# Layer 0 of a two-layer kernel from unit 48 on: engine queues in the source's order, and short consumer steps dealt out over units

## The chip, the cores and the metric

The kernel runs on one core of a Trainium2 chip. The metric is device time in microseconds (us) of one execution, from start to end of the program, as the median of several runs. A profiled execution has a span of its own (first to last recorded instruction), which is used where the working goes into the trace.

## The reference

Two layers act on an input x of 4 batches of 512 tokens with 512 features, held in 16 bits. Each layer normalises x, computes an attention-like branch s and a gate branch g from the normalised input, and adds s * silu(g) to x:

```python
xn = _layernorm(x)
s = _L0_attn_ref(xn, Wq, Wk, Wv, Wo)
g = _silu(_L0_ffn_ref(xn, SU_ug, SU_dp, Wscale_ug, Wscale_dp, W_up, W_gate, W_down))
x = x + s * g
xn = _layernorm(x)
s = _L1_attn_ref(xn, ...)
g = _silu(_L1_ffn_ref(xn, ...))
x = x + s * g
```

Only the first layer is touched by the change. Its two branches are:

```python
# attention: 32 heads of 16 features, 8 key/value heads (4 query heads share one)
attn = jnp.einsum('bhqd,bhkd->bhqk', q, k) * scale
attn = jax.nn.softmax(attn, axis=-1).astype(jnp.float16)
out = jnp.einsum('bhqk,bhkd->bhqd', attn, v)
return out.transpose(0, 2, 1, 3).reshape(b, s, 512) @ Wo
...
# feed-forward: 512 -> 2048 -> 512, with Walsh-Hadamard transforms before both products
x = fwht(x * SU_ug) / SCALE
x_up = x @ W_up.T * (Wscale_ug[:INTER] * SCALE)
x_gate = x @ W_gate.T * (Wscale_ug[INTER:] * SCALE)
x = jax.nn.silu(x_gate) * x_up
x = fwht(x * SU_dp) / SCALE
return x @ W_down.T * (Wscale_dp * SCALE)
```

The second layer is a gated delta-rule recurrence over the tokens with a feed-forward of sign weights.

## The kernel before

**Units.** Layer 0 is dealt out in 256 units (NU, L379): 4 batches x 8 sets x 8 units; a set is the four query heads that share one key/value head, so a batch takes 64 units, and "unit 27 of a batch" means u % 64 = 27. The loop at L544 runs over units and issues for each of them, in this order, what is due:

- *values* (L454), once in eight units: the weighted sum of the values of a whole set, in 16 matmuls from the exponentials into one PSUM bank, a ScalarE copy `os`, and then the chain of *attention sums*: the row sums go out to memory and come back as 128 rows (`rc`), are inverted on VectorE, go out (`rec_d`) and come back spread over all rows (`sm`, four DMAs); GpSimd multiplies `os` by `sm` into `oT`, and four DMAs sort its rows into `oTc`, from which the output product reads. Transfers here are issued by SyncE.
- *maxima* (L422): two matmuls (L429) give scores in `sc`, and VectorE takes the negated row maxima `nmx` (L430).
- *exps* of the unit 11 earlier (LAG): two matmuls with the keys on the rows (L450) into `st`, and ScalarE's exponential `pe` (L452).
- two *halves* of the feed-forward, which trails by 16 units (LATE): 32 units (16 to 47 of the attention's count) compute gate and up products (`gate_up`, L323: "gate units", eight L333 matmuls each; the weights `wc`, four buffers, are loaded by SyncE), the next 32 compute the output product (`down`, L346: "down units", two L351 matmuls each). After a gate product ScalarE takes its tanh `th` and VectorE forms (th + 1) * gate (L340); after an up product ScalarE copies it to `hT` (L343) and GpSimd multiplies the two (L344).
- `max_rows` at the end of a set (L432): VectorE splits the maxima in a 16-bit value and its remainder (`nm`), TensorE transposes them (L439), and VectorE adds them to the queries as two more rows (`qm`, L441), so that the second score product has the maximum already subtracted.
- steps that come once or twice a batch: `queries` (L387), `set_queries` (L412), `layer_sum` of the batch before (L488, four: output product, gate `sg`, sum `x1`), `norm1` (L499, four: statistics of x1 with the first, then normalise, transpose, store), the load and statistics of the next batch's x (`load_x`, `stats0`), its `norm0` (L144, four: normalise, transpose on TensorE, two ScalarE copies `xnT` and `xr`), `keys` (L289) and `values_of` (L303, four). In `norm0` and `norm1` the first of the four also takes the inverse standard deviations: add on VectorE, square root on ScalarE (L68), reciprocal on VectorE.

**PSUM.** `sc` and `st` are one buffer each (two banks), `mm` has three banks and holds the feed-forward's sums; `y` is a single bank, shared by everything else. In a gate unit `keys`, values and `values_of` may take an `mm` bank (`either`, L368) where the feed-forward piece is below 32 of its batch; otherwise they too take `y`.

**Order.** Each engine executes its own queue in order. The order inside a queue is not that of the source: a scheduler in the tile framework places the instructions, by its own estimates of when operands and buffers are ready, unless an instruction is pinned by `keep_in_program_order`, which is used here only for the start (`inorder`, L131) and in layer 1. DMAs are issued from the queue of the engine on which they are called, mostly SyncE (SP).

**Into layer 1.** The feed-forward of the last batch is not done when the units end. What is left of it, and the last batch's `layer_sum` and `norm1`, form the list `rest` (L585), of which entries are dealt out between the steps of layer 1's first batch in proportion to the work done (L876). After them layer 1's own constants are set up; among them `osc` and `drow` come by DMAs from ScalarE's queue (L889 to L895) and are used on VectorE (L902).

Of the kernel before, what the change touches and what calls it, by code (L numbers as in the profile page):

```python
# [18 lines left out]
P = 128  # L19
# [12 lines left out]

@with_exitstack
def kernel(ctx: ExitStack, tc: tile.TileContext, i: dict, out: bass.AP):
    nc = tc.nc
# [18 lines left out]

    def ln_params(pool, rows, tag):

        n = len(rows)
        mv = new(pool, [P, n, 2], F32, tag + "mv")
        for k, r in enumerate(rows):
            st = new(pool, [P, 6], F32, tag + "st")  # L60
            nc.vector.bn_stats(st, r)
            nc.vector.bn_aggr(mv[:, k, :], st)
        return mv, inv_std(pool, mv, n, tag)

    def inv_std(pool, mv, n, tag, pin=lambda ins: ins):
        rstd = new(pool, [P, n], F32, tag + "rs")
        pin(nc.vector.tensor_scalar(rstd, mv[:, :, 1], EPS, None, ALU.add))
        pin(nc.scalar.activation(rstd, rstd, AF.Sqrt))  # L68
        pin(nc.vector.reciprocal(rstd, rstd))
        return rstd  # L70
# [21 lines left out]
    make_identity(nc, identf)  # L92
    ident16 = new(cst, [P, P], F16, "ident16")
    make_identity(nc, ident16)
# [6 lines left out]
    if True:  # L101
# [40 lines left out]
        rstds = {}  # L142

        def norm0(b, pin=lambda ins: ins, then=lambda: None, tiles=range(TB)):  # L144
            xin, mv = xins[b], lnp[b]
            if 0 in tiles:
                xnTs[b] = new(b0, [P, KC, SEQ], F16, "xnT")
                xrs[b] = new(hp, [P, KC, SEQ], F32R, "xr", bufs=1)
                rstds[b] = inv_std(b0, mv, TB, "ln", pin)
            xnT, rstd = xnTs[b], rstds[b]  # L150
            then()
            for t in tiles:
                xn = new(b0, [P, DM], F16, "xn")
                pin(normalize(xn, xin[:, t, :], mv, rstd, t))
                pt = new(bmm, [P, KC, P], F16, "mm") if b == 0 else new(bpy, [P, KC, P], F16, "y")
                for k in range(KC):
                    nc.tensor.transpose(pt[:, k, :], xn[:, ts(k, P)], ident16)
                pin(nc.scalar.copy(xnT[:, :, ts(t, P)], pt))
                if b > 0:
                    nc.scalar.copy(xrs[b][:, :, ts(t, P)], pt)  # L160
            if b == 0:
                for t in range(TB):
                    pin(nc.scalar.copy(xrs[b][:, :, ts(t, P)], xnT[:, :, ts(t, P)]))
# [1312 lines left out]
```

## Time and profile before

| | |
|---|---|
| Median of three runs (1486.90, 1487.87, 1488.85) | 1487.87 us |
| Profiled execution: its time / its span | 1496.22 / 1494.5 us |
| Mean granted TensorE clock of it | 0.985 |
| TensorE busy (matmuls) | 1429.8 us, 96% |
| VectorE busy | 1033.9 us, 69% |
| ScalarE busy | 710.6 us, 48% |
| GpSimd busy | 314.5 us, 21% |
| Memory traffic, mean over the span | 129 GB/s |

The page's groups of instructions list the costliest lines with busy time, mean duration of one, and the idle time of the engine just before them with what ended it. For layer 0 the largest are:

```profile
L430 DVE TENSOR_REDUCE nmx<-sc 128x2 f32<-128x1024 f32 x256 | 312.2, 1220 | 141.3 <-PE st L450 136.2
L452 ACT ACTIVATE pe<-st 128x1024 f16<-128x1024 f32 x256 | 262.6, 1026 | 134.2 <-PE st L450 132.2
L351 PE MATMUL mm<-wdn,hT 128*128 128x512 f32 x512 | 254.4, 618 | 0.0
L333 PE MATMUL mm<-xr,wc 128*128 128x512 f32 x768 | 208.4, 413 | 0.5 <-DMA wc<-wS 0.5
```

A line such as the first reads: line 430, VectorE, a reduction from `sc` to `nmx`, 256 of them, 312.2 us together and 1220 ns each; VectorE had been idle for 141.3 us before them, mostly until a matmul at L450 ended. Idle time of an engine that does not set the pace costs nothing. In the views by time, `PE`, `PEld`, `DVE`, `ACT`, `POOL` and `SP` are TensorE's matmuls, its weight loads, VectorE, ScalarE, GpSimd and SyncE; "[0.47 <-ACT pe]" at the end of a line means that the engine had waited 0.47 us for an ACT instruction on the tile `pe`; in a list of waits stand total, count and the longest. Layer 0 takes the span up to about 830 us; unit 48 starts at about 185 us.

### The profile page before, as it was taken

To read this page: it belongs to the slowest core of one execution; us is meant where nothing else is said; L and a number is where in the kernel's file an instruction comes from. 1 tells how busy PE (TensorE), PEld (TensorE's weight loads), DVE (VectorE), ACT (ScalarE), POOL (GpSimd) and SP (SyncE) were. 2 spreads that over 40 slices of the span, in tenths; PEclk is the share of its full clock that TensorE was granted. 3 is DMA by queue.
4 is the path that set the end of the run, shared out by engine and by line. 5 is a ranking of instruction groups with operands and counts; after the bars stand their busy time and mean duration, and the time that the engine had idled before them with its cause. 6 is when DMAs were issued, how large, how long until landed. Compare 5 with 4: busy or idle time off the path is not lost. (4 is left out here: it accounts for less than half of the span.)

```text
span 1494.5 us, 22672 instructions
## 1 busy us (share of the span) xinstructions
PE 1429.8 (96%) x8144; PEld 859.7 (58%) x8144; DVE 1033.9 (69%) x1863; ACT 710.6 (48%) x1046; POOL 314.5 (21%) x304
## 2 busy tenths in 40 slices
PE   7999999999999999999999699999999999999998
PEld 3456543465335653366335476787568765776675
DVE  7799855756557655676516769668975799477746
ACT  4555554566446664466443434434353344323433
POOL 1022200322003210133110230045112531052001
PEclk9899999999999999999999899999999999999989
DMA  8856310465105640166012543434453354425532
GB/s 294 319 198 227 115 58 23 147 238 191 27 24 201 224 143 27 59 227 222 20 51 80 155 138 106 120 88 137 140 153 105 91 161 135 125 71 148 165 83 96
DMA packets 201793, 199.11 MB, mean 133 GB/s; under 512 B 65520, under 2 KB 153040, under 8 KB 200784
## 3 DMA queue, kind: packets, MB, share of 16 engines
q1 hardware_dynamic: 198624, 196.29, 41.5%
q10 hardware_dynamic: 3056, 1.37, 0.4%
q8 instruction: 64, 1.05, 0.3%
q14 instruction: 49, 0.40, 0.1%
HBM read 146.80 MB, written 46.19 MB: 129 GB/s over the span
## 5 line engine op out<-in xcount | busy, mean ns | idle before, releaser
L430 DVE TENSOR_REDUCE nmx<-sc 128x2 f32<-128x1024 f32 x256 | 312.2, 1220 | 141.3 <-PE st L450 136.2
L452 ACT ACTIVATE pe<-st 128x1024 f16<-128x1024 f32 x256 | 262.6, 1026 | 134.2 <-PE st L450 132.2
L351 PE MATMUL mm<-wdn,hT 128*128 128x512 f32 x512 | 254.4, 618 | 0.0
L333 PE MATMUL mm<-xr,wc 128*128 128x512 f32 x768 | 208.4, 413 | 0.5 <-DMA wc<-wS 0.5
L333 PEld LDWEIGHTS mm<-xr,wc 128*128 128x128 f32 x768 | 138.4, 190 | 49.7 <-issue 22.0
L344 POOL TENSOR_TENSOR hT<-hT,th 128x512 f32<-128x512 f32 x64 | 85.3, 1333 | 317.1 <-ACT hT L343 285.8
L351 PEld LDWEIGHTS mm<-wdn,hT 128*128 128x128 f32 x512 | 86.7, 189 | 90.8 <-issue 90.1
L729 PE MATMUL pu<-xn1T,wp 128*128 128x512 f32 x288 | 131.0, 598 | 0.0
L959 PE MATMUL ph<-xsh,sg 128*128 128x512 f32 x256 | 112.8, 441 | 5.6 <-ACT sg L944 5.3
L429 PE MATMUL sc<-kT,qT 32*128 32x512 f16 x512 | 104.4, 388 | 4.8 <-DVE nmx L430 4.5
L944 ACT ACTIVATE sg<-sw 128x512 fp32r<-128x512 f32 x128 | 79.5, 625 | 56.7 <-PE y L990 29.1
L959 PE MATMUL ph<-xsl,sg 128*128 128x512 f32 x256 | 104.1, 407 | 0.7 <-DVE xsl L919 0.7
L450 PE MATMUL st<-qm,kT 32*128 32x512 f16 x512 | 102.8, 388 | 1.6 <-ACT pe L452 1.6
L476 POOL TENSOR_TENSOR oT<-os,sm 128x512 f16<-128x512 f32 x32 | 41.5, 1297 | 284.7 <-DMA sm<-rec_d 253.1
L429 PEld LDWEIGHTS <-qT 32*128 32x128 f16 x512 | 26.5, 91 | 119.4 <-issue 112.4
L964 ACT ACTIVATE hT<-ph,upsc 128x512 f32<-128x512 f32 x64 | 43.9, 686 | 95.6 <-PE ph L959 95.4
L729 PEld LDWEIGHTS pu<-xn1T,wp 128*128 128x128 f32 x288 | 54.2, 192 | 57.3 <-issue 55.6
L990 PE MATMUL y<-sg,hsh 128*128 128x512 f32 x256 | 82.9, 432 | 0.9 <-ACT sg L944 0.9
L333 PE MATMUL mm<-xr,fo 128*128 128x512 f32 x256 | 75.9, 431 | 0.6 <-DVE fo L260 0.5
L1037 POOL TENSOR_TENSOR gm<-g,le 128x384 fp32r<-128x384 f32 x64 | 57.2, 911 | 89.2 <-PE pu L1038 58.8
L990 PE MATMUL y<-sg,hsl 128*128 128x512 f32 x256 | 73.5, 400 | 0.0
L339 ACT ACTIVATE th<-mm,hwg 128x512 f32<-128x512 f32 x64 | 44.1, 689 | 52.3 <-PE mm L333 49.0
(307 smaller groups left out, 2368.8 us busy)
## 6 DMA issues: line engine op xcount, KB each, us to landing
wc<-wS SPq DMA_DIRECT2D x96, 512.0 KB
wS<-fo SPq DMA_DIRECT2D x16, 1024.0 KB
sw<-in_upT SPq DMA_DIRECT2D x64, 256.0 KB
sw<-in_downT SPq DMA_DIRECT2D x64, 256.0 KB
sm<-rec_d SPq DMA_DIRECT2D x128, 64.0 KB
raw<-in_w_gateT SPq DMA_DIRECT2D x8, 512.0 KB
hT<-in_w_downT SPq DMA_DIRECT2D x16, 256.0 KB
raw<-in_w_upT SPq DMA_DIRECT2D x8, 512.0 KB
```

The source lines that it names most:

```text
L333: nc.tensor.matmul(pgs[m], wcs[b, c, m][:, h, k, :], xrs[b][:, k, :], start=(k + h == 0), stop=(k == KC - 1 and h == 1))
L344: nc.gpsimd.tensor_tensor(hT, hT, ths[b, c], ALU.mult)
L351: nc.tensor.matmul(ys[t], hTs[b, c][:, ts(t, P)], wdn[:, c, :], start=(c == 0), stop=(c == NI - 1))
L429: nc.tensor.matmul(sc[:, j, :], qTs[n][rows, ts(t, P)], kTs[b, g // 4][rows, :], start=True, stop=True)
L430: nc.vector.tensor_reduce(nmxs[n][:, t, 2 * pr : 2 * pr + 2], sc, AX.X, ALU.max, negate=True)
L450: nc.tensor.matmul(st[:, j, :], kTs[b, g // 4][rows, ts(k, P)], qms[n][rows, :], start=True, stop=True)
L452: nc.scalar.activation(pes[u], st, AF.Exp)
L729: nc.tensor.matmul(pp, wps[b, n][:, k, 0:P], xn1Ts[b][:, k, :], start=(k == 0), stop=(k == KC - 1))
L944: tc.keep_in_program_order(nc.scalar.activation(sgs[b, c, m], raws[b, c, m], AF.Sign))
L959: ins = nc.tensor.matmul(ph, sgs[b, c, 0][:, ts(k, P)], xss[b][n][:, k, :], start=(k + n == 0), stop=(k == KC - 1 and n == 1))
L990: ins = nc.tensor.matmul(yss[b][t], hss[b, c][n][:, ts(t, P)], sgs[b, c, 1], start=(c + n == 0), stop=(c == NI - 1 and n == 1))
L1037: nc.gpsimd.tensor_tensor(gm, bc_in(s["g2"][:, t, u, x], P), bc_mid(le, 3), ALU.mult)
```

## The change

From unit 48 on (`FIRST`), every instruction that the unit loop calls on TensorE, VectorE, ScalarE and GpSimd is pinned to the source's order, by a wrapper around the engines (`InOrder`, on while `ordered[0]`); SyncE's DMA issues stay free, and the pinning ends with the loop. The steps of the loop are cut smaller, and what consumes a TensorE or DMA result is deferred by `later(n, f)`, which runs f in the unit n later, after that unit's exps and before its values and feed-forward:

- by one unit: the gate product (th + 1) * gate, the final gate product of `down`, the copies `kd` (with its DMAs), `vp` and `xr`, the addition `qm`, and of `layer_sum` everything after the matmuls (not for the last batch);
- the attention sums in three parts: `os`, its DMA out and `rc` in at once, the reciprocal with `rec_d` and `sm` three units later, the product `oT` with its DMAs five units later;
- `max_rows` is split: the maxima in 16 bits and remainder stay at the end of the set, the transposes (`query_rows`) go to the end of the next unit, `qm` to the one after;
- `norm0` is split in a root (unit 47 of a batch), scale steps (48 to 51) and turns (49 to 52), one a unit; `norm1` in statistics (21 to 24), root (25), scale steps (26 to 29) and turns (27 to 30);
- `queries` moves by one unit (22, 23 of 32), `layer_sum` from 17-20 to 18-21, `keys` from 52 to 53, `values_of` from 56-59 to 57-60; values stands behind exps instead of ahead of maxima.

The list `rest` has the same work in 38 entries instead of 29. No arithmetic is added or left out. The core of the diff:

```diff
+class InOrder:
+    def __init__(self, tc, engine, on):
+        self.tc, self.engine, self.on = tc, engine, on
+    def __getattr__(self, name):
+        f = getattr(self.engine, name)
+        if not self.on[0]:
+            return f
+        return lambda *args, **kw: self.tc.keep_in_program_order(f(*args, **kw))
+class Engines:
+    def __init__(self, tc, on):
+        nc = tc.nc
+        self.tensor, self.vector, self.scalar, self.gpsimd = (
+            InOrder(tc, e, on) for e in (nc.tensor, nc.vector, nc.scalar, nc.gpsimd)
+        )
+        self.sync = nc.sync
 @with_exitstack
 def tile_two_layers_kernel(ctx: ExitStack, tc: tile.TileContext, i: dict, out: bass.AP):
-    nc = tc.nc
+    ordered = [False]
+    nc = Engines(tc, ordered)
...
+        def root(pool, mv, n, tag, pin=lambda ins: ins):
+            rstd = new(pool, [P, n], F32, tag + "rs")
+            pin(nc.vector.tensor_scalar(rstd, mv[:, :, 1], EPS, None, ALU.add))
+            pin(nc.scalar.activation(rstd, rstd, AF.Sqrt))
+            return rstd
+        def norm0_root(b, pin=lambda ins: ins):
+            rstds[b] = root(b0, lnp[b], TB, "ln", pin)
+        def norm0_scale(b, t, pin=lambda ins: ins):
+            if t == 0:
+                pin(nc.vector.reciprocal(rstds[b], rstds[b]))
                 xnTs[b] = new(b0, [P, KC, SEQ], F16, "xnT")
                 xrs[b] = new(hp, [P, KC, SEQ], F32R, "xr", bufs=1)
-                rstds[b] = inv_std(b0, mv, TB, "ln", pin)
-            xnT, rstd = xnTs[b], rstds[b]
-            then()
-            for t in tiles:
-                xn = new(b0, [P, DM], F16, "xn")
-                pin(normalize(xn, xin[:, t, :], mv, rstd, t))
-                pt = new(bmm, [P, KC, P], F16, "mm") if b == 0 else new(bpy, [P, KC, P], F16, "y")
-                for k in range(KC):
-                    nc.tensor.transpose(pt[:, k, :], xn[:, ts(k, P)], ident16)
-                pin(nc.scalar.copy(xnT[:, :, ts(t, P)], pt))
-                if b > 0:
-                    nc.scalar.copy(xrs[b][:, :, ts(t, P)], pt)
-            if b == 0:
-                for t in range(TB):
-                    pin(nc.scalar.copy(xrs[b][:, :, ts(t, P)], xnT[:, :, ts(t, P)]))
+            xns[b, t] = new(b0, [P, DM], F16, "xn")
+            pin(normalize(xns[b, t], xins[b][:, t, :], lnp[b], rstds[b], t))
+        def norm0_turn(b, t, pin=lambda ins: ins):
+            pt = new(bmm, [P, KC, P], F16, "mm") if b == 0 else new(bpy, [P, KC, P], F16, "y")
+            for k in range(KC):
+                nc.tensor.transpose(pt[:, k, :], xns[b, t][:, ts(k, P)], ident16)
+            pin(nc.scalar.copy(xnTs[b][:, :, ts(t, P)], pt))
+            if b > 0:
+                later(1, lambda: nc.scalar.copy(xrs[b][:, :, ts(t, P)], pt))
...
+        waiting, unit = {}, [0]
+        def later(n, f):
+            waiting.setdefault(unit[0] + n, []).append(f)
...
+            def place():
+                kd = new(b0, [P, SEQ], F16, "kd", bufs=1)
+                nc.vector.tensor_copy(kd, pk)
+                for v in range(2):
+                    kT = kTs[b, v] = kTz[2 * (b % 2) + v]
+                    if b + v == 0:
+                        continue
+                    for j in range(4):
+                        nc.sync.dma_start(kT[32 * j + 2 : 32 * j + 2 + HD0, :], kd[ds(64 * v + HD0 * j, HD0), :])
+            later(1, place) if b else place()
...
+                def place(t=t, pv=pv):
+                    nc.vector.tensor_copy(
+                        vp[:, t, :, 0:HD0], pv[:, : NKV * HD0].rearrange("p (h d) -> p h d", d=HD0)
+                    )
+                later(1, place) if b else place()
...
-                nc.scalar.activation(th, pgs[0], AF.Tanh, scale=hwg[:, c : c + 1])
-                nc.vector.scalar_tensor_tensor(th, th, 1.0, pgs[0], ALU.add, ALU.mult)
+                pg = pgs[0]
+                nc.scalar.activation(th, pg, AF.Tanh, scale=hwg[:, c : c + 1])
+                later(1, lambda: nc.vector.scalar_tensor_tensor(th, th, 1.0, pg, ALU.add, ALU.mult))
...
-                nc.scalar.activation(th, ys[t], AF.Tanh, scale=0.5)
-                nc.vector.scalar_tensor_tensor(g0s[b][:, t, :], th, 1.0, ys[t], ALU.add, ALU.mult)
+                y, g = ys[t], g0s[b][:, t, :]
+                nc.scalar.activation(th, y, AF.Tanh, scale=0.5)
+                later(1, lambda: nc.vector.scalar_tensor_tensor(g, th, 1.0, y, ALU.add, ALU.mult))
...
-        NU, LAG, LATE = 8 * len(sets), 11, 16
+        NU, LAG, LATE, FIRST = 8 * len(sets), 11, 16, 48
...
+        def query_rows(n):
+            nmg = nms[n % 2]
             pm = misc(F16)
             for t in range(TB):
                 nc.tensor.transpose(pm[:, ts(t, P)], nmg[:, t].rearrange("p j d -> p (j d)"), ident16)
             qms[n] = new(b0, [P, SEQ], F16, "qm")
-            nc.vector.tensor_tensor(qms[n], pm, qTs[n], ALU.add)
+            later(1, lambda: nc.vector.tensor_tensor(qms[n], pm, qTs[n], ALU.add))
...
+            def invert():
+                nc.vector.reciprocal(rc, rc)
+                nc.sync.dma_start(rec_d[b, g].rearrange("j (p x) -> (j p) x", p=32), rc)
+                for j in range(4):
+                    nc.sync.dma_start(sm[32 * j : 32 * j + 32, :], rec_d[b, g, j : j + 1, :].to_broadcast([32, SEQ]))
+            def place():
+                oT = new(hp, [P, SEQ], F16, "oT")
+                nc.gpsimd.tensor_tensor(oT, os_, sm, ALU.mult)
+                v, r = g // 4, g % 4
+                for j in range(4):
+                    if r == 0 and j % 2 == 0:
+                        oTs[b, 2 * v + j // 2] = new(hp, [P, SEQ], F16, "oTc", bufs=6)
+                    nc.sync.dma_start(
+                        oTs[b, 2 * v + j // 2][ds(64 * (j % 2) + HD0 * r, HD0), :], oT[32 * j : 32 * j + HD0, :]
+                    )
+            later(3, invert)
+            later(5, place)
...
+            def place():
+                sg = new(zp[0], [P, DM], F32, "sg")
+                nc.vector.scalar_tensor_tensor(sg, ps, 0.5, g0s[b][:, t, :], ALU.mult, ALU.mult)
+                x1 = x1s[t] = new(zp[0], [P, DM], F32, "x1", bufs=4)
+                nc.gpsimd.tensor_tensor(x1, sg, xins[b][:, t, :], ALU.add)
+                nc.sync.dma_start(x1_d[tok, :], x1)
+            later(1, place) if b < NB - 1 else place()
...
+        def stats1(b, t):
             if t == 0:
-                mvs[b] = ln_params(zp[0], [x1s[n] for n in range(TB)], "ln")
-            xn1 = new(zp[0], [P, DM], F32, "xn1")
-            normalize(xn1, x1s[t], *mvs[b], t)
+                mvs[b] = new(zp[0], [P, TB, 2], F32, "lnmv")
+            s6 = new(zp[0], [P, 6], F32, "lnst")
+            nc.vector.bn_stats(s6, x1s[t])
+            nc.vector.bn_aggr(mvs[b][:, t, :], s6)
+        def norm1_root(b):
+            rstds[b, 1] = root(zp[0], mvs[b], TB, "ln")
+        def norm1_scale(b, t):
+            if t == 0:
+                nc.vector.reciprocal(rstds[b, 1], rstds[b, 1])
+            xn1s[t] = new(zp[0], [P, DM], F32, "xn1")
+            normalize(xn1s[t], x1s[t], mvs[b], rstds[b, 1], t)
+        def norm1_turn(b, t):
             pt = misc()
             for k in range(KC):
-                nc.tensor.transpose(pt[:, ts(k, P)], xn1[:, ts(k, P)], identf)
+                nc.tensor.transpose(pt[:, ts(k, P)], xn1s[t][:, ts(k, P)], identf)
...
+            if h >= halves(NU + LAG + 1):
+                settle()
+        def settle():
+            for n in sorted(waiting):
+                for f in waiting.pop(n):
+                    f()
...
+            unit[0] = u
+            ordered[0] = u >= FIRST
             if v == 32:
...
-            if 0 < u - LAG <= NU and (u - LAG) % 8 == 0:
-                values((u - LAG) // 8 - 1)
             if u < NU:
                 maxima(u)
             if 0 <= u - LAG < NU:
                 exps(u - LAG)
+            for f in waiting.pop(u, ()):
+                f()
+            if 0 < u - LAG <= NU and (u - LAG) % 8 == 0:
+                values((u - LAG) // 8 - 1)
             for f in early.get(u, ()):
                 f()
             for h in range(halves(u), halves(u + 1)):
                 half(h)
             if u % 8 == 7 and u < NU:
                 max_rows(u // 8)
-            if u % 32 in (21, 22) and u + 11 < NU:
-                queries((u + 11) // 64, (u + 11) % 64 // 32, u % 32 - 21)
+            if u % 8 == 0 and 0 < u <= NU:
+                query_rows(u // 8 - 1)
+            if u % 32 in (22, 23) and u + 10 < NU:
+                queries((u + 10) // 64, (u + 10) % 64 // 32, u % 32 - 22)
             if u % 8 == 0 and u + 8 < NU:
                 set_queries(u // 8 + 1)
             if 16 <= v < 16 + NI:
                 fold_down(v - 16)
-            if 0 < b < NB and r in (17, 18, 19, 20):
-                layer_sum(b - 1, r - 17)
-            if 0 < b < NB and r in (25, 26, 28, 29):
-                norm1(b - 1, (25, 26, 28, 29).index(r))
+            if 0 < b < NB and r in (18, 19, 20, 21):
+                layer_sum(b - 1, r - 18)
+            if 0 < b < NB:
+                if 21 <= r < 25:
+                    stats1(b - 1, r - 21)
+                if r == 25:
+                    norm1_root(b - 1)
+                if 27 <= r < 31:
+                    norm1_turn(b - 1, r - 27)
+                if 26 <= r < 30:
+                    norm1_scale(b - 1, r - 26)
             if b + 1 < NB:
                 if r == 34:
                     load_x(b + 1)
                 if r in (43, 44, 45, 46):
                     stats0(b + 1, r - 43)
+                if r == 47:
+                    norm0_root(b + 1)
+                if 49 <= r < 53:
+                    norm0_turn(b + 1, r - 49)
                 if 48 <= r < 52:
-                    norm0(b + 1, tiles=(r - 48,))
-                if r == 52:
+                    norm0_scale(b + 1, r - 48)
+                if r == 53:
                     keys(b + 1)
-                if 56 <= r < 60:
-                    values_of(b + 1, (r - 56,))
+                if 57 <= r < 61:
+                    values_of(b + 1, (r - 57,))
+        ordered[0] = False
+        settle()
         rest = [(half, h) for h in range(halves(NU + LAG + 1), 2 * NU)]
...
-        rest += [(f, NB - 1, t) for f in (layer_sum, norm1) for t in range(TB)]
+        rest += [(layer_sum, NB - 1, t) for t in range(TB)]
+        rest += [(stats1, NB - 1, t) for t in range(TB)]
+        rest.append((norm1_root, NB - 1))
+        for t in range(TB):
+            rest += [(norm1_scale, NB - 1, t), (norm1_turn, NB - 1, t)]
```

## The prediction

> **What bounds the kernel now.** I read the page first (PE is busy 96% of the span), then the busy time of each engine in stretches cut at every sixteenth row maximum (L430), which makes stretches of 16 units. Of those lines four are enough; after the length of the stretch stand PE, PEld, DVE, ACT and POOL busy, the granted clock, and the DMA share with GB/s.
>
> ```profile
> 363.70:407.80 44.10, 44.04 (x214) 17.69 (x215) 25.01 (x34) 24.01 (x31) 4.64 (x4) 1.00 0.14 43
> 407.80:446.40 38.60, 38.59 (x170) 13.87 (x170) 22.84 (x27) 18.60 (x21) 3.60 (x4) 1.00 0.08 23
> 446.40:500.30 53.90, 50.66 (x272) 30.31 (x271) 38.29 (x64) 34.67 (x46) 15.14 (x13) 0.97 0.59 195
> 675.00:716.40 41.40, 41.40 (x233) 25.69 (x233) 26.06 (x33) 26.31 (x34) 12.84 (x11) 1.00 0.56 189
> ```
>
> Units 112-127 (first line; they hold all of norm0, keys and values_of), 128-143 and 224-239 leave TensorE idle for 0.06 us at most: no order of the queues can shorten them. Only units such as 144-159 (third line; layer_sum and norm1) lose time, and there the clock is also below 1. What can be won is what TensorE waits for from unit 48 on; the whole list of its waits from 185 to 752 us:
>
> ```profile
> PE y L439 <- DVE nm L436: 4.9, 4, 1.8
> PE st L450 <- ACT pe L452: 1.4, 3, 0.6
> PE sc L429 <- DVE nmx L430: 1.0, 1, 1.0
> PE mm L333 <- DMA wc<-wS: 0.5, 2, 0.3
> PE y L284 <- DVE qm L441: 0.2, 1, 0.2
> ```
>
> That is 8.0 us. To it comes the clock; in two stretches of the same view it is half:
>
> ```profile
> 295.06:298.47 3.41, 1.69 (x10) 1.19 (x11) 3.41 (x5) 1.18 (x2) 1.26 (x1) 1.00 0.10 24
> 298.48:301.89 3.41, 3.41 (x12) 1.94 (x11) 1.58 (x5) 3.02 (x5) 0.00 (x0) 0.50 0.73 279
> 475.97:479.38 3.41, 3.41 (x12) 2.12 (x11) 1.40 (x4) 2.38 (x4) 0.00 (x0) 0.50 0.59 201
> 783.12:786.53 3.41, 1.89 (x7) 0.84 (x6) 0.17 (x1) 0.21 (x1) 0.23 (x1) 1.00 0.72 203
> ```
>
> A stretch of 3.41 us with 1.72 us idle (first line) is followed by one at clock 0.50; one with 1.52 us idle (last line; the clock stays 1) is not. Eight L333 matmuls took from 475.70 to 479.20 us at half clock and from 479.59 to 481.57 at full: 3.5 against 2.0, so a half-clock stretch costs 1.5 us. **The most that layer 0 can give back is 8.0 + 2 x 1.5 = 11 us.**
>
> **The change, part by part.** The built program confirms that from unit 48 on each of the four engines follows the source: TensorE runs maxima(u), exps(u-11), values where due, the unit's feed-forward, then the rest; ScalarE exp, due copies, then the copies of this unit's results. SyncE stays free. No work is added except two more table loads in layer 1 (31 instead of 29). So I looked where a first-in-first-out queue now waits.
>
> Unit lengths: two values and two query_rows cost 2 x (0.98 + 0.33) = 2.6 us per 16 units (timeline: values 413.57 to 414.55, transposes L439 to the next matmul 0.33). A down unit is (38.60 - 2.6)/16 = 2.25 us, a gate unit (41.40 - 2.6)/16 = 2.42 us; the four attention matmuls at its head take 0.32 of it. About 0.1 us passes between a producer's last matmul and its reader.
>
> (a) *Sqrt in a pinned ScalarE queue.* Before, the scheduler moved TensorE work into the hole:
>
> ```profile
> 464.87 1.28 ACT L68 ACT_TABLE_LOAD   x1
> 467.41 1.28 ACT L452 ACT_TABLE_LOAD   x1
> 468.49 0.39 PE L429 MATMUL sc<-kT,qT 32*128 32x512 f16 x2
> 468.81 0.50 PE L333 MATMUL mm<-xr,wc 128*128 128x512 f32 x1
> 469.78 0.39 PE L450 MATMUL st<-qm,kT 32*128 32x512 f16 x2 [0.47 <-ACT pe L452]
> ```
>
> Gate work (L333) stands between maxima (L429) and exps (L450), and TensorE lost 0.47 us. Pinned, norm1_root stands at unit 25 of a batch behind the copy hT: 0.1 + 0.59 (L343) + 1.28 + 0.21 (L68) + 1.28 + 1.03 (L452) = 4.49 us after that unit's matmuls `st` is free again. TensorE asks for it in exps of unit 27, one gate unit (2.42) later, and waits 2.1 us with all feed-forward work behind it; three batches: 6.3. norm0_root at unit 47: 4.49 - (2.25 + 0.33) = 1.9 us in unit 49; two batches (the first root, in unit 47, is not pinned): 3.8. The DVE sums feeding Sqrt end earlier (row maximum 1.22, then at most 1.4 more). Sum 10.1 us.
>
> [...]
>
> (b) *One `y` bank, unit 51.* Before:
>
> ```profile
> 370.79 0.59 ACT L158 COPY xnT<-y 128x512 f16<-128x512 f16 x1 [0.46 <-PE y L157]
> 371.00 1.13 PE L351 MATMUL mm<-wdn,hT 128*128 128x512 f32 x2
> 371.27 0.59 ACT L160 CAST xr<-y 128x512 fp32r<-128x512 f16 x1
> 371.75 1.04 ACT L452 ACTIVATE pe<-st 128x1024 f16<-128x1024 f32 x1
> 372.06 1.05 PE L460 MATMUL y<-pe,vp 128*32 128x512 f16 x16
> ```
>
> xr follows xnT at once, and values comes after one of the unit's two down matmuls, so nothing waits. After, xr is due one unit later and behind exp, and values stands ahead of the down matmuls. From the unit's start: 0.1 + 0.59 + 1.03 + 0.59 = 2.3 us until `y` is free, TensorE is there at 0.32: it waits 2.0 us, three batches: 6.0.
>
> (c) *The same bank, unit 59.* The copy vp of the previous unit's values_of is due after this unit's row maximum: 0.45 + 1.22 + 0.29 (L315) = 1.96, less 0.32: 1.65 us, three times: 5.0.
>
> (d) *layer_sum in unit 21.* The bank is freed by sg (L494, 0.69) behind the row maximum and the gate product th (0.67): 0.45 + 1.22 + 0.67 + 0.69 = 3.03, TensorE is there at 2.42: 0.6 x 3. Unit 22's queries wait 0.2 x 2. In units 19 and 20 the longer PE work or the missing th hides it. Sum 2.2.
>
> (e) *Small.* Turns in units 50 and 52 and keys in 53 find `y` free at 2.35 instead of 2.25 (0.1 each); queries in 54 wait for kd behind the reciprocal: 0.45 + 1.22 + 0.24 + 0.69 = 2.6, 0.35. Three batches: 2.0.
>
> (f) *Half clock.* The waits of (a) and (b), eight in all, are 1.9 to 2.1 us long, more than the 1.72 that halved the clock, but must lie almost within one stretch of 3.41 us. I take three, 4.5 us; bounds 0 and 8 x 1.5 = 12.
>
> [...] The row at 295.06 says that 1.7 us is enough.
>
> (g) *Split maxima.* The transposes L439 come one unit after nm, so the 4.9 us go; stats0 no longer runs into norm1, and gate work no longer splits maxima from exps. I credit the full 11 us.
>
> (h) *Attention sums.* They stretch from 12.2 us (os copy to last oTc issue, quiet units) to the fixed five units. For a batch's last set invert is in unit 14, the product in 16; layer_sum reads it at the end of 18. After the reciprocal: rec_d 0.3, landing 1.4, four sm issues 1.75, landing 1.8, product 1.27, four oTc issues 2.4, landing 1.7: 10.6 us. From reciprocal (unit 14, 1.9 us) to the last layer_sum matmul there are 12: covered by 1 us; uncovered it costs its lateness, up to 1.5 us, three times. On SyncE, wc loads for units 27 to 30 stand behind these oTc in unit 25: issued some 2.6 us into it, needed 6.1 us into it, plus the 2.1 us of (a). Taken as 0, bounds 0 and 6.
>
> (i) *Start of layer 1.* The final halves, layer_sum and norm1 are dealt out over 38 entries instead of 29, so they come sooner.
>
> ```profile
> 836.80 1.12 PE L506 MATMUL mm<-identf,xn 128*128 128x128 f32 x8 [4.40 <-DVE xn L73]
> 856.20 1.12 PE L753 MATMUL pu<-identf,yv 128*128 128x128 f32 x4 [5.64 <-DVE yv L742]
> ```
>
> The first wait is DVE's (16.65 of 17 us busy from 825 to 842); its work is only reordered. The second holds 3.19 us in which DVE waited at L902 for osc, whose DMA ScalarE now issues one projection earlier. Gain 3; bounds: 10 lost waits (gain 10), and two more loads of 1.28 with the order against us (loss 4). The rest of layer 1 keeps its order.
>
> Sum: 10.1 + 6.0 + 5.0 + 2.2 + 2.0 + 4.5 - 11 - 3 = **+15.8 us**. It is made against the profiled execution (span 1494.5, its time 1496.2), which ran 8.3 us over the median 1487.9; I carry the difference over: **1503.7 us**.
>
> **Rivals.** *Layer 1 pays for it (faster).* Speaks for it: the two waits above with their 0.72 and the half-clock stretches behind them (5.24 against 3.60 us for eight L729) are worth 4.4 + 0.7 + 5.6 + 2 x 3.4 = 17.5 us, and the halves come sooner. Against: DVE is full there. If all of it went and no clock halved in layer 0: 25.3 - 11 - 17.5 = -3 us, 1485. It decides from a gain of 14 there on. Chance 0.08.
> *The waits overlap (no change).* If half of (a) to (e) hid behind work that I put on the path, 12.6 + 1.5 - 14 = 0, 1488. Against: each wait heads a queue with everything behind it. Chance 0.06. It is also the time if the pinning moved nothing.
> *Half clock everywhere, SyncE late.* (f) at 12 and (h) at 3: +26, 1514. For: the waits exceed 1.72. Against: stretches and waits must line up. Chance 0.16.
> My forecast: 0.70, with its own range 1497 to 1511.
>
> **The numbers.** Within 0.2% (3 us) a measurement of this kernel cannot tell from no change. Slower 0.70 + 0.16 = 0.86, same 0.06, faster 0.08. The range 1494 to 1514 leaves out about 2 in 10.
>
> **What would show it.** After: waits of PE for pe of about 2 us, eleven a run in units 27, 49 (pe), 51 (xr) and 59 (vp), and nm gone from the list; stretches of 16 units near 44 + 6.5 where norm0 stands and unchanged 38.6 and 41.4 elsewhere; clock 0.5 after some of the waits; osc no longer before 856. I am wrong if units 49, 51 and 59 are no longer than their neighbours, or layer 1's start moves by over 10 us.

## The result, and the profile after

The changed kernel takes **1502.61 us** in the median of six runs (1499.1 to 1507.2), the kernel before 1488.22; the ratio is 1.0098 with a 95% interval of 1.0079 to 1.0118. A second set of runs, shown below, gave 1.0085 (1.0069 to 1.0101). By the medians that is 12 to 14 us slower; 15.8 were forecast.

The profiled execution has a span of 1497.5 us, its time is 1499.59. It is only 3.0 us longer than the profiled span before, because that one held a half-clock stretch from 45.9 to 56.1 us that none of the later profiles of this study has, though all run the same work there: units 0 to 15 took 45.7 us in it and 39 to 41 in every other. From here on pinned instructions all carry L41, the line of the wrapper, so groups go by tiles. The list of TensorE's waits from 185 to 770 us (waiter, releaser; total, count, longest):

```profile
PE st L41 <- ACT pe L41: 9.0, 5, 1.8
PE y L41 <- ACT xr L41: 5.3, 3, 1.8
PE y L41 <- DVE vp L41: 4.5, 3, 1.5
PE mm L41 <- DMA wc<-wS: 3.2, 4, 1.5
PE y L41 <- DVE sg L41: 1.3, 3, 0.5
```

The waits for `nm` and `nmx` are gone, and the eleven long waits of the forecast stand there, with their counts. The stretches of 16 units from 112, 128, 144 and 224 (length; PE, PEld, DVE, ACT, POOL busy; clock; DMA share, GB/s), which answer to the four shown of before:

```profile
362.70:411.15 48.45, 43.31 (x213) 17.54 (x213) 24.91 (x35) 26.35 (x34) 4.70 (x4) 1.00 0.13 35
411.15:449.41 38.26, 38.26 (x169) 13.73 (x169) 22.61 (x26) 18.35 (x21) 2.53 (x2) 1.00 0.09 24
449.41:501.50 52.09, 49.81 (x273) 30.73 (x274) 34.21 (x52) 32.57 (x44) 16.13 (x13) 0.97 0.63 203
682.84:723.99 41.15, 40.65 (x233) 25.52 (x233) 26.07 (x32) 25.97 (x35) 12.87 (x10) 1.00 0.60 199
```

Only the first stretch, with norm0, is longer (44.10 before), though TensorE is busy for less of it. How the wait in unit 27 comes about, in the timeline of ScalarE and then of TensorE:

```profile
299.74 0.59 ACT L41 COPY hT<-mm 128x512 f32<-128x512 f32 x1 [0.94 <-PE mm L41]
300.35 1.28 ACT L41 ACT_TABLE_LOAD   x1
301.64 0.20 ACT L41 ACTIVATE lnrs<-lnrs 128x4 f32<-128x4 f32 x1
301.86 1.28 ACT L41 ACT_TABLE_LOAD   x1
303.16 1.02 ACT L41 ACTIVATE pe<-st 128x1024 f16<-128x1024 f32 x1
```

```profile
299.96 2.12 PE L41 MATMUL mm<-xr,wc 128*128 128x512 f32 x8
302.02 0.39 PE L41 MATMUL sc<-kT,qT 32*128 32x512 f16 x2
304.23 0.39 PE L41 MATMUL st<-qm,kT 32*128 32x512 f16 x2 [1.83 <-ACT pe L41]
304.55 0.82 PE L41 MATMUL mm<-pe,vp 128*32 128x512 f16 x10
```

The copy hT, two table loads and the exponential follow one another without a hole, `st` is free at 304.18, and values and all feed-forward work stand behind the waiting pair. The clock that follows:

```profile
301.99:305.40 3.41, 1.58 (x21) 0.52 (x20) 2.35 (x5) 3.40 (x4) 0.00 (x0) 1.00 0.93 347
305.40:308.81 3.41, 3.41 (x12) 2.56 (x9) 0.54 (x2) 0.93 (x2) 0.00 (x0) 0.50 0.65 248
```

The wait lay wholly in one stretch of 3.41 us (1.83 us idle), and the next one ran at half clock. From unit 48 on there are three of these, after unit 27 of each batch; in the second profile three again, after two units 27 and one unit 49.

Cut at the starts of row maxima (of unit 0, 16, 32, 48 and 255), both kernels compare so (us; the second profile of the changed kernel in brackets):

| Part | before | after |
|---|---|---|
| units 0 to 15 | 45.7 | 39.3 (40.5) |
| units 16 to 31 | 52.5 | 53.1 (53.1) |
| units 32 to 47, not pinned | 67.8 | 72.9 (74.4) |
| units 48 to 255 | 567.2 | 575.5 (573.7) |
| of it: waits of TensorE | 8.3 | 23.9 (22.2) |
| of it: everything else | 558.9 | 551.6 (551.5) |
| from there to the end | 742.1 | 737.5 (739.9) |

Two rows were not foreseen: units 32 to 47, which are not pinned in either kernel, became 5 to 7 us longer, and TensorE's own work between units 48 and 255 became 7 us shorter although it holds one half-clock stretch more.

### The profile page after: what moved, and what is told of

Read it like the earlier page. It is cut to its first block, busy times and chain, and to the rows that moved or that the text cites. A ratio compares the mean times of both kernels' runs of the same rounds, so it can differ in the third digit from the quotient of the medians.

```text
span 1497.5 us, 22686 instructions
## 1 busy us (share of the span) xinstructions
PE 1418.5 (95%) x8144; PEld 859.4 (57%) x8144; DVE 1029.8 (69%) x1863; ACT 711.4 (48%) x1048; POOL 312.4 (21%) x304
## 5 line engine op out<-in xcount | busy, mean ns | idle before, releaser
L41 DVE TENSOR_REDUCE nmx<-sc 128x2 f32<-128x1024 f32 x208 | 254.7, 1224 | 216.7 <-PE st L41 216.3
L41 ACT ACTIVATE pe<-st 128x1024 f16<-128x1024 f32 x219 | 224.4, 1025 | 132.3 <-PE st L41 132.3
L41 PE MATMUL mm<-wdn,hT 128*128 128x512 f32 x472 | 235.7, 620 | 0.0
L41 PE MATMUL mm<-xr,wc 128*128 128x512 f32 x768 | 208.6, 415 | 3.4 <-DMA wc<-wS 3.2
L41 PEld LDWEIGHTS mm<-xr,wc 128*128 128x128 f32 x768 | 139.9, 192 | 54.8 <-issue 22.9
L41 PEld LDWEIGHTS mm<-wdn,hT 128*128 128x128 f32 x472 | 79.4, 189 | 84.8 <-issue 84.8
L41 POOL TENSOR_TENSOR oT<-os,sm 128x512 f16<-128x512 f32 x28 | 35.7, 1275 | 314.4 <-DMA sm<-rec_d 253.8
L41 PE MATMUL st<-qm,kT 32*128 32x512 f16 x438 | 84.9, 384 | 9.0 <-ACT pe L41 9.0
L41 POOL TENSOR_TENSOR hT<-hT,th 128x512 f32<-128x512 f32 x48 | 61.9, 1290 | 141.3 <-ACT hT L41 141.2
L41 PE MATMUL sc<-kT,qT 32*128 32x512 f16 x416 | 80.6, 384 | 0.0
L41 PEld LDWEIGHTS <-qT 32*128 32x128 f16 x416 | 19.5, 90 | 87.7 <-issue 82.5
L1046 PEld LDWEIGHTS ph<-xsh,sg 128*128 128x128 f32 x256 | 49.0, 191 | 22.4 <-ACT sg L1031 10.1
```

The lines of the kernel that those rows point to most:

```text
L41: return lambda *args, **kw: self.tc.keep_in_program_order(f(*args, **kw))
L1046: ins = nc.tensor.matmul(ph, sgs[b, c, 0][:, ts(k, P)], xss[b][n][:, k, :], start=(k + n == 0), stop=(k == KC - 1 and n == 1))
```

## The experiments

**The steps without the pinning.**

```diff
-            ordered[0] = u >= FIRST
+            ordered[0] = False
```

> The changed kernel with the pinning taken away and nothing else: the steps stay spread over units, the scheduler orders the queues. Theory (the waits come from pinned queues in front of one st tile and one y bank): TensorE's waits of 1.5 to 1.8 us in units 27, 49, 51 and 59 are gone, TensorE waits from unit 48 on fall from 23.3 us to 12 or less, and the ratio to the kernel before is 0.999 to 1.005 (units 32 to 47, which are not pinned in either kernel and were 5 us longer after the change, stay long). Rival (the deferral by units costs, whatever the order): the ratio stays at 1.008 to 1.012. A second point: maxima and exps are again split by feed-forward matmuls, so TensorE's own work between units 48 and 255, without waits, is back at about 559 us from 552 if the pinned order is what shortened it.

Measured: 1482.54 us against 1491.46, ratio **0.995** (0.9928 to 0.9973): faster than before. The list of TensorE's waits from 190 to 770 us:

```profile
PE sc L458 <- DVE nmx L459: 2.7, 7, 0.6
PE mm L360 <- DMA wc<-wS: 1.2, 1, 1.2
PE st L483 <- ACT pe L485: 0.8, 3, 0.3
```

Units 48 to 255 take 554.4 us, 21.1 less than pinned, with no half-clock stretch among them. So the pinning is what costs, and the deferral by itself gains 12.7 us there; the ratio is below the range expected. Of the 21.1 us, 18.3 are waits of TensorE (23.9 against 5.6) and about 4.5 the three half-clock stretches, while TensorE's own work without these is 1.7 us less in the pinned kernel. The second point of the expectation fell: without waits TensorE's work is 548.8 us and not 559. The steps shorten it, without any pinning.

**The pinning without the steps.** The wrapper of the diff put on the kernel before, from unit 48 on, around its own source order.

> The kernel before, with TensorE, VectorE, ScalarE and GpSimd pinned to its own source order from unit 48 on, without the spread steps. Theory: each step whose consumer stands right behind its producer now stops a queue. The transposes of the row maxima wait for the row maximum and its split in the same unit (1.2 + 0.5 us) in 26 sets, values stands ahead of maxima, and both roots stand with their consumers in one unit: 26 x 1.7 + 7 x 4 = 70 us more, with half clocks on top; ratio 1.04 to 1.08. Rival (pinning is harmless, the steps are what costs): ratio below 1.005.

Measured: ratio **1.1639** (1.1604 to 1.1675); units 48 to 255 take 807 us. The direction was right, the size two to four times too small. TensorE's waits, then VectorE's, from 200 to 1010 us:

```profile
PE sc L41 <- DVE nmx L41: 96.9, 34, 5.2
PE y L41 <- DVE xn L41: 35.8, 13, 4.7
PE y L41 <- DVE nm L41: 35.4, 23, 2.3
```

```profile
DVE rc L41 <- DMA rc<-sum_d: 167.0, 26, 10.4
```

The 35.4 us for `nm` are what had been priced at 26 x 1.7 = 44. What was left out is the reciprocal of the attention sums: pinned right behind values, it holds VectorE's queue for the round trip of the sums through memory, 6.4 us in each of 26 sets, with the row maxima behind it. In the changed kernel, where it comes three units later, the same wait is 0.3 us in all. Beside the waits, 198 of the 807 us ran at half clock, against 6.8 of 567 before.

**The two copies at once.** `xr` and `vp` lose their `later(1, ...)`.

```diff
-                later(1, lambda: nc.scalar.copy(xrs[b][:, :, ts(t, P)], pt))
+                nc.scalar.copy(xrs[b][:, :, ts(t, P)], pt)
...
-                later(1, place) if b else place()
+                place()
```

> The changed kernel, but the copies xr (norm0) and vp (values_of) are not deferred: each stands behind its own matmuls again, everything else pinned as before. Theory: the waits for the y bank in units 51 (xr, 5.3 us) and 59 (vp, 4.5 us) go, nothing takes their place (ScalarE has both copies done 1.3 us after the end of the unit, st is free 2.3 us after it, TensorE asks for it at 2.4), so 9.8 us less than the changed kernel: ratio 1.0032. Rival (the next thing is late instead: TensorE waits for st in units 50 to 53, or for sc behind vp): the two waits go and others come, ratio 1.007 or more.

Measured: ratio **1.005** (1.0029 to 1.0071). Waits from 190 to 770 us:

```profile
PE st L41 <- ACT pe L41: 9.0, 5, 1.8
PE mm L41 <- DMA wc<-wS: 3.4, 7, 0.9
PE y L41 <- ACT xr L41: 2.5, 3, 0.8
PE y L41 <- DVE sg L41: 1.3, 3, 0.4
```

The wait for `vp` is gone, that for `xr` fell from 1.75 to 0.83 us (xnT and xr still take 1.2 us after the turn, values asks 0.3 us into the unit), and nothing took their place: 7.3 us of waits less where 9.8 were expected, and 5 to 7 us in the ratio. Four stretches from unit 48 on ran at half clock in this profile, against three in the changed kernel.

**The roots on GpSimd.** For a pinned root:

```diff
-            pin(nc.scalar.activation(rstd, rstd, AF.Sqrt))
+                nc.gpsimd.tensor_scalar(rstd, v, -0.5, 1.5, ALU.mult, ALU.add)
+                for _ in range(3):
+                    nc.gpsimd.tensor_tensor(y, rstd, rstd, ALU.mult)
+                    nc.gpsimd.tensor_tensor(y, y, v, ALU.mult)
+                    nc.gpsimd.tensor_scalar(y, y, -0.5, 1.5, ALU.mult, ALU.add)
+                    nc.gpsimd.tensor_tensor(rstd, rstd, y, ALU.mult)
```

> The changed kernel, but the two roots that are pinned (norm1 in unit 25, norm0 in unit 47 of the later batches) are worked out by 14 small GpSimd instructions (three Newton steps from 1.5 - 0.5 v) in place of Sqrt on ScalarE and the reciprocal on VectorE. Theory: no table loads there, so the waits for pe in units 27 and 49 go (9.0 us), and with them the three half-clock stretches that follow unit 27 (3 x 1.5): 13.5 us less than the changed kernel, ratio 1.001. Rival 1 (the half clock comes anyway, from other waits): 9 us less, ratio 1.004. Rival 2 (GpSimd is too slow, VectorE's scale step waits for it with the row maxima behind): the waits for pe turn into waits for nmx or xn and the ratio stays above 1.007.

Measured: ratio **1.0099** (1.0072 to 1.0126), no gain. The waits for `pe` are gone altogether, and other waits stand in their place, as the second rival has it:

```profile
PE y L41 <- DVE qm L41: 8.3, 2, 4.1
PE mm L41 <- DMA wc<-wS: 6.0, 5, 2.2
```

```profile
368.06 1.35 DVE L41 TENSOR_SCALAR xn<-xin,lnmv,lnrs 128x512 f16<-128x512 f16 x1 [4.37 <-POOL lnrs L41]
369.34 1.21 DVE L41 TENSOR_REDUCE nmx<-sc 128x2 f32<-128x1024 f32 x1
```

The first list names `qm`, but VectorE's timeline shows what was late: the scale step `xn` of unit 48 waited 4.37 us for GpSimd's root, and the row maximum, `qm` and the transposes were behind it. The 14 small instructions came about 0.28 us apart, 4.0 us in all. Three of the waits for `wc` (0.87, 0.75 and 0.73 us) are in unit 27 of three batches; the first of them:

```profile
305.94 2.12 PE L41 MATMUL mm<-xr,wc 128*128 128x512 f32 x8 [0.87 <-DMA wc<-wS]
```

These loads are issued behind the `oTc` transfers of unit 25 in both kernels; in the changed kernel TensorE was waiting for `pe` at that time, which hid them. Behind the new waits five stretches of 3.41 us ran at half clock instead of three. So Sqrt caused the waits for `pe`; a root that is late for VectorE costs as much.

**Deferral only from unit 48 on**, without pinning:

```diff
 def later(n, f):
-    waiting.setdefault(unit[0] + n, []).append(f)
+    if unit[0] < FIRST:
+        f()
+    else:
+        waiting.setdefault(unit[0] + n, []).append(f)
```

> No pinning, and steps deferred only from unit 48 on: before that, what is deferred runs at once, as in the kernel before (the transposes of the maxima still come one unit later). Theory: the 1.8 us wait in unit 41 (TensorE's y bank held by qm) and the half-clock stretch behind it come from the deferral in units that were full already, so units 32 to 47 take 68 to 70 us instead of 74.5 and the whole 3 to 6 us less than with the steps alone: ratio 0.991 to 0.993. Rival (the transposes one unit later are what hurts there): units 32 to 47 stay at 73 or more, ratio 0.995.

Measured: ratio **0.9921** (0.9899 to 0.9943); units 32 to 47 take 67.9 us. In the changed kernel the list for these units begins with the first line, here with the second:

```profile
PE y L299 <- DVE qm L474: 1.8, 1, 1.8
```

```profile
PE y L299 <- DVE qm L477: 1.2, 2, 1.0
```

In units 32 to 43 the weights are still being mixed, and VectorE's queue is full (busy 55.7 of 58.1 us before, 51.8 of 60.0 in the changed kernel); `qm` one unit later holds the `y` bank for 1.8 us, and a half-clock stretch follows (155.2 to 158.7 us in the changed kernel, gone here). The intervals of the times of this kernel and of the steps alone overlap, so the gain isn't shown in the time. In the units it is: the seven profiles with the early deferral have 72.9 to 74.5 us there, the three in which it begins at unit 48 (two of them further down) 67.9 to 70.6.

**One step alone**: in the kernel before, the transposes and `qm` one unit after the split of the maxima, nothing else.

> The kernel before, and one step of the change alone: the transposes of the row maxima and qm one unit after the split of the maxima, no pinning. Theory: this one step carries most of what the spread steps gain between units 48 and 255 (12.7 us): the 4.9 us of waits for nm go, and TensorE's own work falls from 559 towards 550 us because the transposes no longer stand between maxima and exps; units 48 to 255 take 555 to 560 us, ratio 0.994 to 0.997. Rival (the gain comes from the norms, gates and attention sums): units 48 to 255 stay above 563 us, ratio 0.998 to 1.001.

Measured: ratio **0.9972** (0.9955 to 0.999); units 48 to 255 take 560.4 us, of which 551.4 without waits, just outside both ranges of the expectation. So this step brings 6.8 of the 12.7 us, but not by fewer waits: those for `nm` are gone, others stand in their place, and the sum is 9.0 us where it was 8.3. The longest is now:

```profile
PE sc L429 <- DVE nmx L430: 4.0, 5, 1.1
```

TensorE's own work is 7.5 us less; 3 of these are the two half-clock stretches, and 1 is work that moved across the cut. What the step changes is seen in the kernel before, in unit 87:

```profile
294.61 0.39 PE L429 MATMUL sc<-kT,qT 32*128 32x512 f16 x2
294.61 0.39 PE L450 MATMUL st<-qm,kT 32*128 32x512 f16 x1
296.78 0.40 PE L439 MATMUL y<-ident,nm 128*128 128x128 f16 x4 [1.78 <-DVE nm L436]
297.11 0.38 PE L450 MATMUL st<-qm,kT 32*128 32x512 f16 x1
```

The transposes stand between the two matmuls of exps. Taken over units 48 to 255 from starts of matmuls (next start less the wait): a matmul of maxima costs 0.003 us if exps follow at once, since the two then run side by side (both start at 294.61 above), and 0.318 if transposes over the full array follow. Not all of the 0.318 is the change: a `wo` product, 16 bits and 512 columns too, costs 0.216 us ahead of another one, and 0.312 ahead of maxima. Changes between attention matmuls on a part of the array and matmuls on all of it number 454 before, 442 with this step, 414 in the changed kernel; the matmuls just ahead of a change to the full array cost 71.9, 70.2 and 65.6 us. Each change costs about 0.1 us, in either direction (0.318 and 0.312 less 0.216); the rest of those sums is time of attention matmuls that no neighbour shares.

**TensorE free, the other three engines pinned** (`self.tensor = nc.tensor` in the wrapper).

> The changed kernel with TensorE left to the scheduler and VectorE, ScalarE and GpSimd pinned. Theory: the waits cost because TensorE's queue has the waiting matmul in front of work that is ready; with that queue free most of the eleven long waits shrink below 0.6 us and the ratio is 0.995 to 1.001. Rival (the results come late for every order of TensorE's queue, since ScalarE and VectorE are what is pinned wrong): the waits stay, ratio 1.006 to 1.011.

Measured: ratio **0.9994** (0.9975 to 1.0013); of the waits from 190 to 770 us these lead:

```profile
PE mm L361 <- DMA wc<-wS: 5.1, 5, 1.6
PE sc L459 <- DVE nmx L41: 1.5, 3, 0.7
```

All eleven long waits are gone with ScalarE's and VectorE's queues unchanged. Unit 27 of the second batch, ScalarE and TensorE:

```profile
301.63 0.59 ACT L41 COPY hT<-mm 128x512 f32<-128x512 f32 x1 [0.93 <-PE mm L361]
304.22 1.04 PE L494 MATMUL mm<-pe,vp 128*32 128x512 f16 x14
305.05 1.02 ACT L41 ACTIVATE pe<-st 128x1024 f16<-128x1024 f32 x1
306.66 0.39 PE L484 MATMUL st<-qm,kT 32*128 32x512 f16 x2
```

From the copy `hT` to the exponential pass 3.42 us, as in the changed kernel (299.74 to 303.16): the results are no earlier, but TensorE has other work in front, here values. Units 48 to 255 take 563.5 us, so 12 of the 21 us that the pinning costs come back.

**All mends together, pinned.** Copies at once, `sg` and `x1` at once, roots on GpSimd with two steps (10 instructions) in units 24 and 46.

> The changed kernel, pinned as it is, with the places mended at which TensorE waited: copies xr and vp at once, sg and x1 of layer_sum at once, and the pinned roots by 10 small GpSimd instructions (0.285 us apart in the last run of that kind) one unit earlier (units 24 and 46; the first, in unit 46 of the first batch, keeps Sqrt). Theory (these waits and the half clocks behind them are all that the pinning costs): 1.0098 less 7.1 us for the copies, 9.0 us for the waits for pe, 4.5 for three half clocks and 1.3 for sg = 22 us, ratio 0.995, the same as without pinning. Rival (a queue in source order loses time elsewhere too): ratio 0.999 or more, with other waits in the list.

Measured: ratio **0.9925** (0.9903 to 0.9947), 24 to 26 us less than the changed kernel where 22 were expected. The longest waits:

```profile
PE mm L41 <- DMA wc<-wS: 3.2, 5, 1.1
PE y L41 <- ACT xr L41: 2.5, 3, 0.8
```

Units 48 to 255 take 551.2 us, without a half-clock stretch, and TensorE's own work is 544.0 us, less than in any unpinned kernel here (548.8). So a pinned queue need not be slower, and the account of the 21.1 us above has nothing beside waits and clock. But the mends weren't put on the kernel without pinning; how much of the 24 to 26 us they would gain there isn't shown.

**The changed kernel once more, the mends with late deferral, and a fifth `wc` buffer**, in one set of runs. The first is the changed kernel, the second has the mends and the `later` shown above, the third differs from the second by `bufs=5` for `wc`.

> The changed kernel itself once more, beside the same runs of the kernel before as the two below: ratio 1.008 to 1.012, the same eleven waits of 1.5 to 1.8 us in units 27, 49, 51 and 59 and a half-clock stretch behind unit 27 of each batch. What differs from the first profile of it is then what one execution differs from another by: the stretches of half clock elsewhere.

> The mended pinned kernel, with the deferral only from unit 48 on. Theory (the two mends are independent: units 32 to 47 lose 74.2 - 67.9 = 6.3 us, half of it seen in the time of the unpinned pair, 2.4 to 6 us): ratio 0.988 to 0.991, units 32 to 47 at 68 us and units 48 to 255 at 551 us. Rival (in the pinned kernel the units before 48 leave more for the first pinned ones, or layer 1 takes it back): ratio 0.9925 as before.

> The same with five buffers for the feed-forward weights wc instead of four. Theory (the waits of TensorE for wc, 2.9 us in the mended kernel, come from loads that are issued behind the oTc transfers on SyncE with too little ahead): with one more load ahead the waits for wc fall below 0.5 us, 2 to 3 us less, ratio 0.986 to 0.989. Rival (the order on SyncE decides, not the number of buffers): the waits stay and so does the time.

Measured: 1.0085 (1.0069 to 1.0101) for the changed kernel, with the same eleven waits, but half clock came behind unit 27 in two batches only, and once behind unit 49; **0.9916** (0.9894 to 0.9938) for the second; 0.9937 (0.9917 to 0.9957) for the third. In the second, units 32 to 47 came to 70.6 us instead of 68, with a half-clock stretch in them, what follows unit 255 took 747.2 us (742.9 in the mended kernel), and its time can't be told from that of the mended kernel: that fits the rival, and this gain wasn't shown in the time. In the third, TensorE's waits from 185 to 740 us and VectorE's timeline show a new wait:

```profile
PE sc L41 <- DVE nmx L41: 5.1, 4, 2.4
PE y L41 <- ACT xr L41: 2.5, 3, 0.8
PE mm L41 <- DMA wc<-wS: 1.0, 3, 0.5
```

```profile
354.17 0.25 DVE L41 RECIPROCAL rc<-rc 128x16 f32<-128x16 f32 x1 [3.56 <-DMA rc<-sum_d]
```

The waits for `wc` fell from 2.5 to 1.0 us, and the reciprocal of the sums came 3.56 us late on VectorE instead, with the row maxima behind it: neither expectation. SyncE issued the row sums' way out 5.0 us after the start of the copy `os` here (342.77 to 347.75), behind `oTc` and `wc`, and 0.7 us after it with four buffers (343.99 to 344.65): with other loads its transfers fall in another order, and another one is late.

Six versions here beat both kernels. The four fastest can't be told from one another: steps deferred from unit 48 without pinning (0.9921), the mended pinned kernel (0.9925), that with late deferral (0.9916, 1476.0 us) and with five buffers as well (0.9937). The steps alone (0.995) and the one step (0.9972) are the other two.

## Why the prediction was right

The forecast of 1503.7 us, its sign and its reason (a pinned queue waits where a scheduler had filled the hole) hold. The sum came out by more than its own terms, though. Step by step:

- *(a) Sqrt*: 10.1 forecast, 8.97 measured, 1.83 and 1.74 us a wait, in the units named, three and two times. The order of ScalarE's instructions was as worked out; TensorE asked 0.3 us later. Taking Sqrt away took these waits away. In the timeline above the two table loads take 1.28 us each, and 0.02 us at most lie between copy, loads, Sqrt and exponential.
- *(b), (c) one bank*: 6.0 and 5.0 forecast, 5.25 and 4.53 measured (1.75 and 1.51 us, three times each); undoing the two deferrals removed 7.3 of the 9.8.
- *(d) layer_sum*: 2.2 forecast, 1.35 measured (0.45 in unit 21; unit 22 waits for nothing that the list shows). *(e)*: 2.0 forecast, nothing above 0.15 us found. Both were mis-sized upwards, by 0.1 to 0.35 us at each place, where the margin was as small.
- *(f) half clock*: three stretches forecast, three found in both profiles, where they vary between places. Three was taken between bounds of 0 and 8; that it was met is luck. If the stretches of 3.41 us are counted on from those at half clock, all five waits of 1.83 us in the two profiles that lie in one stretch were followed by half clock, but only one of three waits of 1.74 to 1.75 us that do, and none of 1.51 us or split over two stretches. The 1.72 us of the prediction is no threshold, then; the rows at 301.99 and 305.40 show that 1.83 us was enough there.
- *(g)*: the waits of 8.0 us and the two half-clock stretches are gone, as credited. **Not foreseen** is that TensorE's own work falls with it: 558.9 us with two half-clock stretches against 551.6 with three, so by 7.3 + 1.5 = 9 us; the cost ahead of changes to the full array accounts for 6.3 of it, the 20 changes back to a part for about 2, and 1 us is work of unit 47 that moved across the cut. That the transposes wedged between maxima and exps cost time even without a wait was not priced. With it falls the bound: the prediction says that layer 0 can give back 11 us at most and that no order shortens units in which TensorE is never idle. Units 48 to 255 became 12.7 us shorter with the steps alone and 16.0 in the mended kernel.
- *(h)*: the row of the list for `wc` shows 3.2 us (1.7 in the second profile), where 0 was taken and 0 to 6 left open. The mechanism was the one named, on SyncE behind oTc, but in units 36, 37 and 45, not 27 to 30. In unit 27 the wait of (a) covered the lateness, as the text had it: without Sqrt up to 0.87 us of it show.
- *(i) start of layer 1*: gain of 3 forecast. In the 125 us after the last row maximum TensorE's waits fall from 14.3 to 11.3 us; the wait for `yv` from 5.64 to 4.08, and VectorE no longer waits for `osc` (3.19 before), as named there. The whole remainder is 2.2 to 4.6 us shorter, with the clock in it.
- *Left out of the sum*: units 32 to 47. The text counted the pinned units alone, but the deferral acts from the first unit, and costs 5 to 7 us there.

From unit 48 to 255 the sum's terms give +18.8 (all but the start of layer 1), measured are +8.3 and +6.6; the missing 10 to 12 us are (g)'s unforeseen 9 and the smaller waits of (a) to (e), 5 us, less the 3.2 of (h). Units 32 to 47 give 5 to 7 back. So two errors of opposite sign stand behind a total that is 1 to 4 us off, and that it came so close is in part luck. Carrying the sum over to the median of the runs was right, since what set the profiled execution 8.3 us apart was mostly the half-clock stretch at its start (6.4 us in units 0 to 15).

Of the rivals, the full overlap is refuted by the list of waits; layer 1 gave 2 to 5 us and not 14; half clock everywhere did not come.

## What to carry to other kernels

A queue in source order is only as good as the slack of each of its steps: list for every single-buffered tile when its reader ends and when the next writer asks, and give a step whose operand makes a round trip through memory its units of delay before the order is pinned. Spreading and pinning are two changes and want two measurements: here one gains 0.5%, the other takes away 1.5% and, mended at four places, takes nothing. Count the changes between matmuls on a part of the array and matmuls on all of it, and the small matmuls that lose their neighbour, as well as the waits.

## What the runs showed of the hardware

A change between matmuls on a part of the array and matmuls on all of it cost about 0.1 us in either direction (0.312 against 0.216 us for a `wo` product ahead of maxima, and 0.318 for a matmul of maxima ahead of transposes). A matmul of maxima cost 0.003 us with a neighbour to run beside and 0.318 without. GpSimd took 0.20 us for an operation on 128x4, and issued dependent ones about 0.28 us apart. Half clock followed an idle 1.83 us in a stretch of 3.41 each time, an idle 1.74 to 1.75 us in some cases only, and two executions of one kernel had it behind different waits. The six runs of the changed kernel spread over 8 us, with granted clocks of 0.981 to 0.987; how much of the spread is the clock isn't separated.
